# Two fused graph layers: the last batch's projections by seven block products, and buffers of its own for the last pair

## The chip, the cores and the metric

The kernel runs on one core of a Trainium2 chip. The metric is device time in microseconds for one execution, of which the kernel before has three runs (the median is used). The core's engines are TensorE (PE, with its weight loads shown as PEld), VectorE (DVE), ScalarE (ACT), GpSimd (POOL) and SyncE (SP), which here issues the transfers. Each engine works through its own queue in order.

## The reference, cut to what matters

There are 64 graphs of 256 nodes with 256 features. Layer 0 is a convolution over the nodes, a message passing step and a gated update. Layer 1, which is what the change touches, is this (after the layer norm, `h` is the normalised `x`):

```python
def _L1_gnn_ref(x, adj, W_rel, b_rel, W_root, ln_gamma, ln_beta):
    h = layer_norm(x, ln_gamma, ln_beta)
    agg = jnp.einsum('bij,bjh->bih', adj, h)
    conv = jnp.einsum('bkh,ho->bko', agg, W_rel) + b_rel + jnp.einsum('bkh,ho->bko', h, W_root)
    return x + jax.nn.relu(conv)
...
x = _layernorm(x + _L0_gnn_ref(x, adj, ...), axis=-1)
x = _layernorm(x + _L1_gnn_ref(x, adj, ...), axis=-1)
```

Everything is in float32.

## The kernel before, in words

**Tiles and stages.** The 64 graphs are eight batches of eight. Each batch is first convolved over its nodes in a transformed domain (`conv`): the data lie in 48 slots of 128 x 256 in a tile `XF`, whose slots are called `X`, and 47 filter matrices are multiplied in (`product`, `ps_k`, L735), streamed from DRAM through `cs`. Then the batch's graphs are taken in pairs; `pair(p)` records the work of graphs 2p and 2p+1 for p = 0 to 31, so the last batch is the pairs 28 to 31. While one batch's pairs are worked on, the next batch's convolution runs between them; in the last batch there is no next one, and the slots of `X` are unused once the pair's convolved rows have been copied to `XC`.

**A pair** takes these steps, each with the line of its recording:
- messages (`ps_msg`, L1118), distances from node coordinates that make a trip through DRAM (`ps_dist`, L1154), the adjacency `AT` (an exponential on ACT, times the mask on DVE, L1161), and the neighbour sum `nmp` (`ps_nmp`, L1168);
- the gates. Two blocks per side of weights and features are multiplied by seven products in place of eight (Winograd's form of Strassen's method), in the tiles `RG` and `ZN`: `product` L1220 accumulates into PSUM banks `ps_a`, `ps_b`, `ps_d`; `put` copies a bank out on ACT (L1232 for `ZN`, L1234 for `RG`), `onto` adds one on DVE (L1238), `squash` is a tanh (L1242). A bank `ps_a` is used for four products in succession, each accumulated onto the one before, and each must have been copied out before the next starts. Pairs 0, 1 and 31 are "plain": they use eight ordinary products (`ps_g`, L1206);
- the update (L1302 to L1311), which leaves the new state transposed in `wT`;
- `norm`: the statistics of the new state. From pair 2 on, `wT` is turned by a DVE transpose within 32 x 32 blocks (L1328, into `HY`) and two trips through DRAM (`wd`, L1332, and back to `x1`, L1336). In the last batch ("late") the statistics are bn_stats on DVE (`stats`, L1092 and L1093); q and the shift `sh` follow through a power on POOL (L1370) and L1372, and L1376 on ACT scales `x1`;
- `project`: `HY = (wT.T @ [W_rel, W_root]) * q + hrow`, with the two weight matrices side by side in `wrr`. For each graph and half of its nodes (`spots`) there are two matmuls of 128 x 128 by 128 x 512 into `ps_hy` (L1395), and DVE scales the bank into `HY` (L1397);
- `aggregate`: the mask `adja` (loaded at L1315) times the first half of `HY` (`ps_agg`, L1409), an addition (L1412), relu and residual (L1413), statistics, L1428 and L1431 with a power on POOL (L1429), the scaling on ACT (L1438), and the store (L1439).

**The last pair** ("apart") is done block by block. Its graph 0 passes the gates ahead of its graph 1, and each block is finished by `turn_in` (L1247 to L1253: three steps on DVE, two tanh on ACT, then three on DVE). PE transposes `wT` (`ps_wT`, L1350), the projection is L1386 with its scaling L1389, and graph 1's two halves of nodes are aggregated one by one in `last_nodes` (L1448 to L1458).

**What sets the order.** All operations are first recorded as `Op`s with a key, which is a due time computed from the constants at the top: `FIRST_GATES + p * PERIOD` is a pair's due time, `LATE_LAG` shifts the last batch's projections and aggregations behind their own gates, `LOAD_AHEAD` shifts loads, and so on. `scheduled` is a list scheduler with assumed durations, which picks for each engine the ready operation with the smallest key; DVE operations of a pair get a lead. What it returns is the fixed order of each engine's queue, and it also assigns the eight PSUM banks. So a constant changes no operation, only the order in which the operations stand in the queues.

Buffers: `x1`, `HY`, `wT` and `adja` are one tile each, used by all pairs in turn.

Of the kernel before, what the change touches and what calls it, by code (L numbers as in the profile page):

```python
# [18 lines left out]
P = 128  # L19
B, N, D = 64, 256, 256  # L20
C = D // P
# [33 lines left out]
OB, OG = 3, 64  # L55
HQ = 2 * M * C * (M + 1)
XC_SLOTS = BG + 2
FIRST_GATES, PERIOD, GATE_TIME = 112.8, 58.9, 14.5
AHEAD_FROM, AHEAD_TO, W_DEEP = -31.4, -60.1, 2
CONV1_FROM, CONV1_TO, CONV_FROM, CONV_OUT, CONV_TO = -29.4, 98.8, -11.5, -38.6, -37.2  # L60
PAIR_LEAD, FILTER_LEAD, LOAD_AHEAD = 40.4, 0.1, 17.5
SMALL_RUNS, TURN_FROM = 1.3, 2
FILTERS_TO, STORES_AT = 51.4, 46.6
KEEP = 13.0
LATE_LAG = 28.1
W_FROM, W_LAG = 2, 43.3
COORDS = 39.9
PLAIN, SUMS_FROM = (0, 1, B // 2 - 1), 2


# [349 lines left out]
def gnn_two_layers(  # L420
# [18 lines left out]
    prog = Program()  # L439
    PE, V, A, G, SP = prog.tensor, prog.vector, prog.scalar, prog.gpsimd, prog.sync  # L440
# [3 lines left out]
    def sb(name, shape, pool="const"):  # L444
        s = Space(name, shape, pool)
        s.after = opened.get(pool)
        spaces[pool].append(s)
        return s.view

    def ring(name, shape, n, pool="const"):  # L450
        return cycle([sb(f"{name}{i}", shape, pool) for i in range(n)])

    def bank(name, share="rest"):
        return Space(name, [P, 512], "psum", share, share if share in ("conv", "gate") else None).view

    def stt(o, in0, s, in1, op0=ALU.mult, op1=ALU.add, up=1):
        V.scalar_tensor_tensor(o, in0, s, in1, op0=op0, op1=op1, lines_up=up)
# [25 lines left out]
    X = XF[:, :SLOTS * D].rearrange("p (s e) -> p s e", e=D)  # L483
# [494 lines left out]
    wrr = sb("wrr", [P, C, 2 * D])  # L978
    hrow = sb("hrow", [P, 2 * D])
# [58 lines left out]
    wT = sb("wT", [P, 4, N], "work")  # L1038
    x1 = sb("x1", [P, 2, C, D], "work")
    HY = sb("HY", [P, 2, C, 2 * D], "work")  # L1040
    XC = sb("xc", [P, C, XC_SLOTS, N], "work")
    adja = sb("adja", [P, 2, C, N], "work")

    while next(first) != 0:
        pass
# [24 lines left out]
    ps = bank("ps_hrow")  # L1070
# [10 lines left out]
    ps = bank("ps_mean")  # L1081
# [3 lines left out]
    for c in range(C):  # L1085
        stt(wrr[:, c, :], ps, -1.0 / D, wrr[:, c, :])

    mvs, sixes = ring("mv", [P, 4, 2], 2), ring("six", [P, 6], 2)

    def stats(mv, src):  # L1090
        six = next(sixes)
        V.bn_stats(six, src)  # L1092
        V.bn_aggr(mv, six)  # L1093

    qs, q3s = ring("q", [P, 2, 4], 2), ring("q3", [P, 4], 2)
    shs, totals = ring("sh", [P, 4], 4), ring("total", [P, 4], 8)
    sqs, nss = ring("sq", [P, C, 2, 3], 2), ring("ns", [P, C, 2], 2)

    def pair(p):
# [13 lines left out]
        for g in range(2):  # L1113
            for m in range(C):
                ps = bank("ps_msg")
                with prog.group():
                    for c in range(C):
                        PE.matmul(ps[:, :D + 4], xT[:, c, g, m * P:(m + 1) * P], wms[:, c, :], start=(c == 0),  # L1118
                                  stop=(c == C - 1), hold=[msg[:, g, m]])
# [16 lines left out]

        prog.at(due - COORDS, 0.3)
        V.transpose(turned.rearrange("p m e -> p (m e)"), st.rearrange("p m e -> p (m e)"))
# [11 lines left out]
        with prog.group():  # L1150
            for g in range(2):
                for m in range(C):
                    r = slice((2 * g + m) * SR, (2 * g + m) * SR + 4)
                    PE.matmul(pss[2 * g + m][:, :N], lr[r, 0, m * P:(m + 1) * P], lr[r, 1, :], start=True, stop=True,  # L1154
                              hold=[AT[:, g, m]])
# [7 lines left out]
        for g in range(2):  # L1163
            ps = bank("ps_nmp")
            with prog.group():
                for d in range(C):
                    for m in range(C):
                        PE.matmul(ps[:, d * N:(d + 1) * N], msg[:, g, m, d * P:(d + 1) * P], AT[:, g, m, :],  # L1168
                                  start=(m == 0), stop=(m == C - 1), hold=[nmp[:, :, g]])
# [8 lines left out]
        for v, t, when in zip(ins, (tx, nmps, tc_), (due - 28, due - 10, due - 20)):  # L1178
            prog.at(when, 0.3)
            b11, b12, b21, b22 = (v[:, c, g, :] for c in range(C) for g in range(2))  # L1180
# [42 lines left out]

        prog.lead = PAIR_LEAD
        late = p >= B // 2 - BG // 2
        plain = p in PLAIN
        apart = p == B // 2 - 1

# [26 lines left out]
        if plain:  # L1255
            prog.at(due, 2 * GATE_TIME / 44)
            for gs in ((0,), (1,)) if apart else ((0, 1),):
                for T in (RG, ZN):
                    for f in range(C):
                        for g in gs:  # L1260
                            a = bank("ps_g", "gate")
# [8 lines left out]
        else:  # L1270
            for T in (RG, ZN):
                second = T is ZN
                prog.at(due + second * GATE_TIME, GATE_TIME / 21)
                a = bank("ps_a", "gate")
                product(a, 0, second, True)
                put(T, 0, 0, a)
                b_ = bank("ps_b", "gate")
# [4 lines left out]
                d = bank("ps_d", "gate")  # L1282
# [17 lines left out]
        for some in pieces:  # L1300
            r, gh, z, n = (T[:, some, h, :] for T in (RG, ZN) for h in range(2))
# [15 lines left out]
        def spots(gs):  # L1317
            return [(g, m, 2 * g + m) for g in gs for m in range(C)]

        def norm(gs):  # L1320
# [55 lines left out]
                A.activation(x1[:, g, m, :], source[j], AF.Identity, bias=sh[:, j:j + 1], scale=q[:, 0, j:j + 1])  # L1376
            return q

        def project(gs, q):
            prog.at(due + 2 * GATE_TIME + (8 if not apart else -6 if gs[0] else 13 - 2 * GATE_TIME) + (0.0 if apart or p < W_FROM else LATE_LAG if late else W_LAG), 0.6)  # L1380
            if apart:
                pss = [bank("ps_hy") for _ in range(C)]
                for f in range(C):
                    with prog.group():
                        for g, m, j in spots(gs):
                            PE.matmul(pss[m], wT[:, 2 * f + g, m * P:(m + 1) * P], wrr[:, f, :], start=(f == 0),  # L1386
                                      stop=(f == C - 1), hold=[HY[:, g, m]])
                for g, m, j in spots(gs):
                    stt(HY[:, g, m, :], pss[m], q[:, 1, j:j + 1], hrow)  # L1389
                return  # L1390
            for g, m, j in spots(gs):
                ps = bank("ps_hy")
                with prog.group():
                    for f in range(C):
                        PE.matmul(ps, wT[:, 2 * f + g, m * P:(m + 1) * P], wrr[:, f, :], start=(f == 0),  # L1395
                                  stop=(f == C - 1), hold=[HY[:, g, m]], need=[q[:, 1, j:j + 1]])
                stt(HY[:, g, m, :], ps, q[:, 1, j:j + 1], hrow)  # L1397

        def aggregate(gs):
            prog.at(due + 2 * GATE_TIME + (16 if not apart else 14 - 2 * GATE_TIME) + (0.0 if apart or p < W_FROM else LATE_LAG if late else W_LAG), 0.4)  # L1400
            q, sh = next(q3s), next(shs)
# [58 lines left out]
        if apart:  # L1460
            for gs in ((0,), (1,)):
                q = norm(gs)
                project(gs, q)
            aggregate((0,))
            last_nodes()
        else:
            q = norm((0, 1))
            project((0, 1), q)
            aggregate((0, 1))
# [3 lines left out]
    for b in range(NB):  # L1473
        for p in range(b * BG // 2, (b + 1) * BG // 2):
            if p == B // 2 - 1 and p in PLAIN:
                prog.at(FIRST_GATES + (p - 2) * PERIOD, 0.01)
                A21[0] = X[:, :5].rearrange("p s e -> p (s e)")[:, :9 * P].rearrange("p (s g e) -> p s g e", s=3, g=3)
                for s, (src, r) in enumerate(((whhT, 0), (wihT, D), (wihT, 0))):
                    SP.dma_start(out=A21[0][:, s], in_=src[r:r + P].rearrange(
                        "p (g h e) -> p g h e", g=3, h=2)[:, :, 1, :])  # L1480
            pair(p)
            prog.lead = 0.0
            if p + 1 == SUMS_FROM:
                weight_sums(FIRST_GATES + p * PERIOD + 12)
        if b + 1 < NB:
            start, span = FIRST_GATES + b * BG // 2 * PERIOD, BG // 2 * PERIOD
            at1 = len(prog.ops)
            coming = conv(b + 1)
            while next(coming) != "out":
                pass  # L1490
            at2 = len(prog.ops)
            at3 = at2
            while next(coming) != 0:
                pass
            at3 = len(prog.ops)
            spread(at1, at2, start + CONV_FROM, start + span + CONV_OUT)
            spread(at2, at3, start + span + CONV_OUT, start + span + CONV_TO)
            keep(coming, start + span + CONV_TO)
            at3 = len(prog.ops)
            if b + 2 < NB:  # L1500
                conv1(b + 2)
                spread(at3, len(prog.ops), start + CONV1_FROM, start + CONV1_TO)
# [83 lines left out]
```

## Time and profile before

| | before |
|---|---|
| runs, median (lowest to highest) | 1985.53 us (1984.71 to 1985.73) |
| profiled execution, its own time | 1985.06 us |
| its span, first to last instruction | 1983.3 us |
| granted PE clock | 0.999 |
| PE busy, DVE busy, ACT busy | 1968.8, 1714.0, 1009.2 us |
| projection `ps_hy` L1395, PE | 224.3 us in 496 records |
| `ps_agg` L1409, PE | 118.4 us in 504 records |
| scaling L1397, DVE | 124 instructions, 748 ns each |

The profile is of one execution. A float32 matmul appears as two records, its two passes. Busy times of PE are from modelled ends, so that a record is longer (593 ns for 512 columns) than the distance to the next one; the chain of waits gives the distances. Times in a timeline are microseconds from the start of the span.

### The profile page before, as it was taken

The numbers are of one execution on the slowest core, as the hardware profiler recorded it, in microseconds if no ns is written. First come the engines' busy times: TensorE is split into PE (matmuls) and PEld (weight loads), VectorE is DVE, ScalarE is ACT, GpSimd is POOL, SyncE is SP. The second block draws the span as 40 slices with busy tenths as digits, with TensorE's granted clock in tenths as the row PEclk, the third lists the DMA queues.
The fourth block names the chain that finished last, engine by engine and source line by source line (L and its number), as shares of the span: only waits on it lengthen the run. The fifth ranks groups of instructions, "written<-read, shape, count | busy, mean of one in ns | idle before, by whom it ended". The sixth has DMA issues, their size and how long they took to land.

```text
span 1983.3 us, 28889 instructions
## 1 busy us (share of the span) xinstructions
PE 1968.8 (99%) x10196; PEld 1602.8 (81%) x10196; DVE 1714.0 (86%) x2674; ACT 1009.2 (51%) x2342; POOL 290.8 (15%) x512
## 2 busy tenths in 40 slices
PE   9999999999999999999999999999999999999998
PEld 6877789777887788878887788877898788887875
DVE  6996998999999998999989999899988999995655
ACT  7545443654446543664346544475445653456432
POOL 2111110211111111112011111112111010111001
PEclk9999999999999999999999999999999999999999
DMA  8863554446554554445544455544545325422221
GB/s 222 296 209 101 160 155 132 136 114 183 134 153 129 131 181 127 129 141 156 169 142 126 125 146 166 155 131 109 170 136 153 97 81 166 126 73 77 76 54 43
DMA packets 461104, 273.12 MB, mean 138 GB/s; under 512 B 258208, under 2 KB 445600, under 8 KB 460960
## 3 DMA queue, kind: packets, MB, share of 16 engines
q1 hardware_dynamic: 460400, 270.94, 47.7%
q8 instruction: 80, 1.31, 0.3%
q14 instruction: 64, 0.52, 0.1%
q10 hardware_dynamic: 560, 0.34, 0.1%
HBM read 194.01 MB, written 77.20 MB: 137 GB/s over the span
## 4 chain that ended last, share of the span: by engine, by line
PE 96%; ACT 2%; DVE 1%; DMA 1%; issue 0%; SPq 0%; POOLq 0%; POOL 0%; DVEq 0%; ACTq 0%
PE ps_a L1220 23%; PE ps_k L735 17%; PE ps_d L1220 11%; PE ps_hy L1395 11%; PE ps_b L1220 6%; PE ps_nmp L1168 6%; PE ps_agg L1409 5%; PE ps_msg L1118 5%; PE ps_c L879 5%; PE ps_g L1206 4%; PE ps_dist L1154 1%; ACT w2all L596 1%; ACT tT L571 1%; DMA cs<-w2m 0%; PE ps_hy L1386 0%
## 5 line engine op out<-in xcount | busy, mean ns | idle before, releaser
L735 PEld LDWEIGHTS ps_k<-XF,cs 128*128 128x128 f32 x2632 | 311.1, 192 | 15.5 <-issue 10.2
L735 PE MATMUL ps_k<-XF,cs 128*128 128x128 f32 x2632 | 313.1, 275 | 0.0
L1395 PE MATMUL ps_hy<-wrr,wT 128*128 128x512 f32 x496 | 224.3, 593 | 0.0
L1220 PE MATMUL ps_a<-nmp,WB 128*128 128x256 f32 x696 | 207.0, 379 | 0.0
L1395 PEld LDWEIGHTS ps_hy<-wrr,wT 128*128 128x128 f32 x496 | 92.3, 190 | 93.0 <-issue 86.5
L1220 PE MATMUL ps_a<-tx,WB 128*128 128x256 f32 x522 | 155.2, 381 | 2.0 <-ACT ZN L1232 2.0
L1232 ACT COPY ZN<-ps_a 128x512 f32<-128x512 f32 x116 | 67.7, 584 | 172.4 <-PE ps_a L1220 172.0
L1220 PEld LDWEIGHTS ps_a<-nmp,WB 128*128 128x128 f32 x696 | 132.2, 190 | 18.0
L1234 ACT ACTIVATE RG<-ps_a,bhh 128x512 f32<-128x512 f32 x116 | 79.2, 683 | 122.8 <-PE ps_a L1220 120.3
L707 DVE TENSOR_TENSOR XF<-XF 128x512 f32<-128x512 f32 (+3 forms) x128 | 126.6, 1010 | 8.5 <-ACT XF L788 6.6
L1118 PE MATMUL ps_msg<-wms,xT 128*128 128x260 f32 x512 | 133.2, 383 | 0.0
L1397 DVE SCALAR_TENSOR_TENSOR HY<-ps_hy,q,hrow 128x512 f32<-128x512 f32 x124 | 92.8, 748 | 36.3 <-PE ps_hy L1395 22.1
L1168 PE MATMUL ps_nmp<-AT,msg 128*128 128x256 f32 x512 | 119.1, 379 | 0.0
L1409 PE MATMUL ps_agg<-HY,adja 128*128 128x256 f32 x504 | 118.4, 379 | 0.0
L1409 PEld LDWEIGHTS ps_agg<-HY,adja 128*128 128x128 f32 x504 | 95.1, 190 | 25.7 <-issue 14.4
L1220 PEld LDWEIGHTS ps_a<-tx,WB 128*128 128x128 f32 x522 | 96.2, 190 | 23.8 <-issue 7.4
L1423 POOL TENSOR_SCALAR total<-total 128x4 f32<-128x4 f32 x28 | 13.4, 478 | 655.7 <-ACT HY L1419 640.1
L1168 PEld LDWEIGHTS ps_nmp<-AT,msg 128*128 128x128 f32 x512 | 96.8, 190 | 13.8 <-DVE AT L1161 0.5
L1118 PEld LDWEIGHTS ps_msg<-wms,xT 128*128 128x128 f32 x512 | 94.8, 190 | 14.5 <-issue 2.4
L879 PE MATMUL ps_c<-xTc,w 128*128 128x512 f32 x232 | 106.3, 593 | 0.0
L1220 PE MATMUL ps_a<-xc,WB 128*128 128x256 f32 x348 | 103.5, 379 | 0.0
L1220 PE MATMUL ps_a<-tc,WB 128*128 128x256 f32 x348 | 103.5, 379 | 0.0
(227 smaller groups left out, 4360.1 us busy)
## 6 DMA issues: line engine op xcount, KB each, us to landing
cs<-w2m SPq DMA_DIRECT2D x105, 768.0 KB
adjm<-in_adjT_dram SPq DMA_DIRECT2D x64, 256.0 KB
xT<-xt SPq DMA_DIRECT2D x32, 512.0 KB
adja<-in_adjT_dram SPq DMA_DIRECT2D x64, 256.0 KB
out_dram<-HY SPq DMA_DIRECT2D x63, 256.0 KB
hd<-xn SPq DMA_DIRECT2D x28, 544.0 KB
XF<-hd SPq DMA_DIRECT2D x28, 544.0 KB
xt<-xTc SPq DMA_DIRECT2D x29, 512.0 KB
```

Of the source, the lines that this page charges most:

```text
L707: (V.tensor_add if add else V.tensor_sub)(sl(o, n), sl(a, n), sl(b, n))
L735: PE.matmul(ps[:, o * P:(o + 1) * P], w(m, c)[:, o * P:(o + 1) * P], X[:, slot, c * P:(c + 1) * P], start=first and o == 0 and c == 0, sto ...
L879: PE.matmul(ps, w1[:, c, o * P:(o + 1) * P], xTc[:, c, :], start=(c == 0), stop=(c == C - 1), hold=[h[:, :, o]])
L1118: PE.matmul(ps[:, :D + 4], xT[:, c, g, m * P:(m + 1) * P], wms[:, c, :], start=(c == 0), stop=(c == C - 1), hold=[msg[:, g, m]])
L1168: PE.matmul(ps[:, d * N:(d + 1) * N], msg[:, g, m, d * P:(d + 1) * P], AT[:, g, m, :], start=(m == 0), stop=(m == C - 1), hold=[nmp[:, :, g]])
L1206: PE.matmul(ps[:, h * N:(h + 1) * N], block[:, s, gate, :], right[s][2 * k + g], start=0 in ks and h == 0 and s == sources[0] and k == 0, ...
L1220: PE.matmul(ps[:, h * N:(h + 1) * N], block[:, s, gate, :], right[s][at], start=start and h == 0 and j == 0, stop=j == len(sources) - 1, s ...
L1232: A.copy(o, ps)
L1234: A.activation(o, ps, AF.Identity, bias=bhh[:, 2, f:f + 1])
L1395: PE.matmul(ps, wT[:, 2 * f + g, m * P:(m + 1) * P], wrr[:, f, :], start=(f == 0), stop=(f == C - 1), hold=[HY[:, g, m]], need=[q[:, 1, j: ...
L1397: stt(HY[:, g, m, :], ps, q[:, 1, j:j + 1], hrow)
L1409: PE.matmul(ps[:, n_ * D:(n_ + 1) * D], adja[:, g, m, n_ * P:(n_ + 1) * P], HY[:, g, m, :D], start=(m == 0), stop=(m == C - 1))
```

## The change

Three things change together.

1. For the pairs from `SEVEN_FROM` = 28 on, other than the last, `project` calls the new `seven_products`: the 2 x 2 blocks of `wT` and of `wrr` are multiplied by seven block products of 256 columns. Sums of weight blocks are made once (`wrr_sums`), differences of state blocks for each pair; they lie in free slots of `X` (29 to 36). The products go to three banks (`ps_ha` four times, `ps_hb`, `ps_hd` twice), are copied or added into `HY`, and `HY` is scaled in place.
2. In the last pair, `x1`, `HY`, `wT` and `adja` are slots 8 to 27 of `X`; the rings of small tiles (`mv`, `six`, `q`, `q3`, `sh`) are longer.
3. Fifteen or so of the constants that make the keys have other values, so that the queues' orders differ.

```diff
-FIRST_GATES, PERIOD, GATE_TIME = 112.8, 58.9, 14.5
-AHEAD_FROM, AHEAD_TO, W_DEEP = -31.4, -60.1, 2
-CONV1_FROM, CONV1_TO, CONV_FROM, CONV_OUT, CONV_TO = -29.4, 98.8, -11.5, -38.6, -37.2
-PAIR_LEAD, FILTER_LEAD, LOAD_AHEAD = 40.4, 0.1, 17.5
+FIRST_GATES, PERIOD, GATE_TIME = 111.7, 58.8, 14.3
+AHEAD_FROM, AHEAD_TO, W_DEEP = -31.2, -63.8, 2
+CONV1_FROM, CONV1_TO, CONV_FROM, CONV_OUT, CONV_TO = -25.7, 97.3, -11.5, -38.6, -36.1
+PAIR_LEAD, FILTER_LEAD, LOAD_AHEAD = 40.4, -0.5, 19.5
 SMALL_RUNS, TURN_FROM = 1.3, 2
-FILTERS_TO, STORES_AT = 51.4, 46.6
+FILTERS_TO, STORES_AT = 50.9, 52.3
 KEEP = 13.0
-LATE_LAG = 28.1
+LATE_LAG = 38
 W_FROM, W_LAG = 2, 43.3
-COORDS = 39.9
+COORDS = 43.5
+SEVEN_FROM = B // 2 - 4
...
+    SHARED = x1, HY, wT, adja
...
+    made_sums = []
+
+    def wrr_sums():
+        a11, a12, a21, a22 = (wrr[:, k, f * D:(f + 1) * D] for f in range(2) for k in range(C))
+        s2, s4, s5, s6 = (X[:, i] for i in range(29, 33))
+        if not made_sums:
+            kept = prog.key, prog.step
+            prog.at(FIRST_GATES + SEVEN_FROM * PERIOD + 40, 0.01)
+            V.tensor_add(s4, a21, a22)
+            V.tensor_sub(s5, s4, a11)
+            V.tensor_sub(s6, a11, a21)
+            V.tensor_sub(s2, a12, s5)
+            prog.at(*kept)
+            made_sums.append(1)
+        return a11, a12, s2, a22, s4, s5, s6
+
-    mvs, sixes = ring("mv", [P, 4, 2], 2), ring("six", [P, 6], 2)
+    mvs, sixes = ring("mv", [P, 4, 2], 6), ring("six", [P, 6], 12)
...
-    qs, q3s = ring("q", [P, 2, 4], 2), ring("q3", [P, 4], 2)
-    shs, totals = ring("sh", [P, 4], 4), ring("total", [P, 4], 8)
+    qs, q3s = ring("q", [P, 2, 4], 4), ring("q3", [P, 4], 4)
+    shs, totals = ring("sh", [P, 4], 8), ring("total", [P, 4], 8)
...
+        x1, HY, wT, adja = SHARED
+        if p == B // 2 - 1:
+            x1 = X[:, 8:12].rearrange("p (g m) d -> p g m d", g=2)
+            HY = X[:, 12:20].rearrange("p (g m h) d -> p g m (h d)", g=2, m=C)
+            wT, adja = X[:, 20:24], X[:, 24:28].rearrange("p (g c) n -> p g c n", g=2)
...
+        def seven_products(q):
+            b11, b12, b21, b22 = (wT[:, i] for i in range(4))
+            t = X[:, 33:37]
+            V.tensor_sub(t[:, 0:2], wT[:, 1:4:2], wT[:, 0:2])
+            V.tensor_sub(t[:, 2], b22, t[:, 0])
+            V.tensor_sub(t[:, 3], b21, t[:, 2])
+            blocks = (b11, b21, b22, t[:, 3], t[:, 0], t[:, 2], t[:, 1])
+            w_ = wrr_sums()
+
+            def one(ps, i, start):
+                with prog.group():
+                    for m in range(C):
+                        PE.matmul(ps[:, m * D:(m + 1) * D], blocks[i][:, m * P:(m + 1) * P], w_[i],
+                                  start=start and m == 0, stop=True, skip_group_check=True,
+                                  hold=[HY] if i == 0 else [], need=[q[:, 1]] if start else [])
+
+            def place(f, g, ps, add):
+                o, v = HY[:, g, :, f * D:(f + 1) * D], ps.rearrange("p (m d) -> p m d", m=C)
+                V.tensor_add(o, o, v) if add else A.copy(o, v)
+            a = bank("ps_ha")
+            one(a, 0, True)
+            place(0, 0, a, False)
+            b_ = bank("ps_hb")
+            one(b_, 1, True)
+            place(0, 0, b_, True)
+            one(a, 5, False)
+            place(0, 1, a, False)
+            d = bank("ps_hd")
+            one(d, 4, True)
+            one(a, 6, False)
+            place(1, 1, a, False)
+            place(1, 1, d, True)
+            one(d, 2, False)
+            place(0, 1, d, True)
+            one(a, 3, False)
+            place(1, 0, a, False)
+            for g, m, j in spots((0, 1)):
+                stt(HY[:, g, m], HY[:, g, m], q[:, 1, j:j + 1], hrow)
...
+            if p >= SEVEN_FROM:
+                seven_products(q)
+                return
```

## The prediction

> **What bounds the kernel now.** I read the profile's page first: TensorE (PE) is busy 99% of the span, VectorE (DVE) 86%, and DVE falls to five or six tenths in the last slices, where no convolution is left.
>
> ```profile
> PE 1968.8 (99%) x10196; PEld 1602.8 (81%) x10196; DVE 1714.0 (86%) x2674; ACT 1009.2 (51%) x2342; POOL 290.8 (15%) x512
> DVE  6996998999999998999989999899988999995655
> ```
>
> A busy PE may still hide gaps, so next comes the table of busy time by stretch, and against it the sum of PE's work from the chain of waits (a 256-column pass every 0.216 us, a 512-column one every 0.43). From 145.6 us, PE's one wait of 1.4 us behind the weight set-up (`ps_mean`), to the end of its last unbroken run at 1972, the passes sum to 1817 of 1826 us. What is missing is some 31 times 0.19 us behind `ps_dist` (the products after its small matmuls take 2.35 in place of 2.16) and three stalls of 0.9 us. So the middle has nothing to win, and any new wait of PE there is paid in full.
>
> ```profile
> 150.00:1780.00 1630.00, 1629.33 (x8315) 1334.95 (x8314) 1464.14 (x2215) 832.62 (x1974) 243.41 (x427) 1.00 0.48 137
> 1930.00:1984.00 54.00, 44.37 (x176) 32.11 (x174) 29.37 (x85) 14.12 (x28) 6.82 (x7) 0.96 0.17 47
> ```
>
> (Line numbers are always those of the kernel before. Columns: stretch, length, then busy time and count of PE, PEld, DVE, ACT, POOL, then PE's clock.) Then the chain of waits, in order of time (start, length, what), around the change and to the end:
>
> ```profile
> 1862.85 3.45 PE ps_agg L1409 x16
> ...
> 1911.80 0.59 ACT ZN L1232
> 1912.39 0.04 issue
> 1912.44 2.43 PE ps_a L1220 x10
> ...
> 1943.76 6.87 PE ps_hy L1395 x16
> ...
> 1958.62 4.32 PE ps_g L1206 x20
> ...
> 1980.00 0.60 ACT HY L1457
> ```
>
> Eight projection matmuls of 512 columns (16 passes) take 6.87 us; 16 passes of 256 take 3.45; and where a bank's next product follows directly on the one that ACT must first copy out, PE stands. Last, DVE's timeline (start, length, instruction) for how its instructions follow one another at the end:
>
> ```profile
> 1970.51 0.69 DVE L1412 TENSOR_TENSOR HY<-HY,ps_agg 128x512 f32<-128x512 f32 x1 [1.55 <-PE ps_agg L1409]
> 1971.31 0.69 DVE L1413 SCALAR_TENSOR_TENSOR HY<-HY,x 128x512 f32<-128x512 f32 x1
> 1972.04 0.43 DVE L1092 BATCH_NORM_STATS2 six<-HY 128x6 f32<-128x256 f32 x1
> ...
> 1973.24 0.17 DVE L1428 TENSOR_SCALAR q<-mv 128x2 f32<-128x2 f32 x1
> 1973.32 0.15 DVE L1372 SCALAR_TENSOR_TENSOR sh<-mv,q 128x2 f32<-128x2 f32 x1
> 1973.39 1.40 DVE L1389 SCALAR_TENSOR_TENSOR HY<-ps_hy,q,hrow 128x512 f32<-128x512 f32 x2
> ```
>
> Add, relu, four statistics and the small step take 2.7 us of DVE per graph; two evictions of 512 take 1.3.
>
> **1. The products.** Per pair 16 passes of 512 (6.87) become 28 of 256: 28 x 0.216 = 6.04 us. That is 0.83 less, in pairs 28, 29 and 30: **-2.49 us**, all of it PE time. Here a rule speaks against it: the Trainium skill ("TensorE: Matmul & The Clock Gate", Back-to-back issue gap) says that spacing is set by weight load and matmul together, 81 ns at 128 columns and 131 at 512. Interpolated to 98 ns at 256, an estimate, 28 would cost 2.7 against 2.1 and the three pairs would lose 1.9 us; this trace's 256- and 512-column rows are strictly proportional.
>
> **2. What the products add elsewhere.** Per pair on DVE: three differences (0.69 + 2 x 0.42), three additions from PSUM (0.69 each) and four scalings from SBUF in place of four from PSUM (0.7 each, even); on ACT four copies of 0.58; once, four sums of weights (0.42 each). In pairs 28 and 29 DVE (30 of 50 us busy) and ACT (20 of 50) take this beside PE: 0. But each `ps_ha` copy stands between two products of one bank, and what is queued on PE behind a waiting product waits too. In the built order other matmuls lie between, at least one 0.86 us product, against a copy of 0.58 and two handovers. That just fits in pair 29's projection; there, though, a copy also comes between ACT's four exponentials, and pair 31's `ps_nmp` follows `ps_dist` by 2.6 us with an `AT` that I reckon 0.25 late, 0.45 with the restart: **+0.45** (0 to 2.8, three full stalls).
>
> **3. The gates' own adjacency.** In the built order of before a gate product follows its own bank's copied one three times; after, four times. Each costs 0.65 waiting and 0.27 (2.43 against 2.16) restarting: **+0.92**.
>
> **4. The constants.** PE's order is the same through pair 4's gates, so the filters are untouched; a few swaps differ up to pair 9, then the distances from `ps_dist` to `ps_nmp` and from `ps_hy` to `ps_agg` repeat those of before. SP's queue is reshuffled from the 79th transfer (a filter load ahead of the `hd` store, `sd` ahead of `xn` and `XF`); the wait at 145.6 is DVE's queue and stays. I take 0; below by 0.4 (all that is unexplained in the middle), above by 1.4, one such wait.
>
> **5. The last pair's buffers.** They free pair 31 from pair 30's `wT`, `HY`, `x1`, `adja`. No wait of PE in the trace is for these: the mask was issued at 1962.2 and used at 1968.6 without one. By itself 0. What it allows is the new order, with `LATE_LAG` 38: pair 30's projection and aggregation are interleaved with pair 31's gates and last steps. One step is moved in DVE's queue: pair 30's transpose (L1328) stood at 1926.8, before pair 31's `turn_in`; now it is behind the first of them, some 7.5 us later, and its two trips through DRAM (9.8 us before, transpose's end to landing) bring `x1` at about 1945.4. Its statistics stand in DVE's queue ahead of pair 31's first evictions, whose products PE ends at 1947.2, so there is a margin of about 1 us: I take 0, up to 2 if the transfers slip.
>
> **6. The end.** Count from the last gate product. Before it ends at 1962.78 (start of the next instruction) and the span at 1983.3: 20.5 us. Behind it lie 11.0 us of PE work before and 13.4 after (two of pair 31's projections, 3.44, have moved ahead; three of pair 30's products, 2.59, and its two aggregations, 3.45, have come behind, less 0.2 of transposes). So after it ends earlier by 2.40 + 2.49 - 0.92 - 0.45 = 3.5 us, at 1959.3. From there, in the built order, with the steps just shown (us behind that point):
>
> - DVE and ACT turn the last block (L1248 to L1253, done at 3.4); PE's last `ps_ha` ends at 3.7, ACT's copy at 4.45. From here DVE no longer waits.
> - first scaling, four statistics and two small steps on the last `ps_wT`, the `ps_hd` addition, two scalings: 4.5 to 8.4.
> - graph 0 of pair 31 (add, relu, four statistics, small): to 11.2.
> - two evictions of graph 1, pair 30's first add between: to 13.2. `ps_agg` L1448 needs both, and waits 3.3 us on PE.
> - graph 0 of pair 30, rest: to 15.1; the fourth scaling: 15.7; node half 0 of graph 1: 17.45; node half 1's add: 17.8.
> - graph 1 of pair 30: to 20.4; node half 1's relu and statistics: 21.7; POOL's power (0.55) and the shift: 22.6.
> - ACT has pair 30's four scalings (2.06) queued in front of the last L1457: from 22.0 to 24.6. Before, the end came 2.7 behind that instruction; with two 256 KB stores just ahead I add 0.4: 27.7.
>
> The last node half before had DVE almost for itself; now pair 30's 10 us of late work stand in its queue. The end grows from 20.5 to 27.7: **+7.2 us** (26.3 if stores and handovers cost nothing, 29 if each of ten handovers costs 0.13 more).
>
> **Sum.** -3.5 + 7.2 = +3.7 on the span of 1983.3, so 1987.0; the profiled execution took 1985.06, 1.8 outside the span, and the median of the runs is 1985.53, 0.5 above that: 1985.53 + 3.7 = **1989.2 us**.
>
> **The rivals.** *DVE keeps up and the end stays PE's* (not slower): if DVE clears pair 30's scalings and first aggregate before the last gate product, PE ends at 1959.3 + 13.4 + 0.2 = 1972.9; then 2.7 (graph), 1.3 (power and shift), 2.1 (ACT), 2.7 (store): 1981.7, so -1.6, 1983.9. It decides once DVE's unbroken queue behind the last gate product is 5.3 us shorter than I counted (13 in place of 18 us); against it, all those steps stand in one queue in the order above, and only a wrong duration could shorten it. *PE waits in the projections too*: three stalls of 0.92 more, or `x1` 2 us late, give 1991 to 1992. For it, the margins of 0.1 and 1 us; against, ACT is 40% busy there. *The seven products do not save*: with loads in the way, +2.5 on my sum, 1991.7; 256-column rows speak against it. *Something in the middle is faster*: the accounting leaves 0.4 us, so I know no mechanism; if I misread DVE's end as well, 1981.
>
> **Chances.** My case 0.60, the PE-bound end 0.15, waits in the projections 0.18, an unseen gain 0.07. A measurement of this kernel tells about 0.2%, 4 us, from no change. My case straddles +4 us, nearly half of it above; the second lies within, the third above: faster 0.07, same 0.47, slower 0.46. The range reaches from most of the PE-bound end to the late `x1`: 1984.5 to 1992.0; my case's own is 1987.2 to 1991.2.
>
> **What would show it.** Right: `ps_ha`, `ps_hb`, `ps_hd` at 0.216 us a pass; four PE waits on `ZN` L1232; PE's wait before the last-node `ps_agg` grown from 2.0 to about 3.3 and now on DVE; DVE without idle time over its last 18 us; the last gate product near 1959. Wrong: that product above 1961 (waits in the projections), or DVE idle in the last 15 us and the span below 1984.

## The result and the profile after

Eleven runs of the changed kernel have a median of 1990.37 us (1989.75 to 1991.12), eleven of the kernel before, on the same chip, 1985.23 us (1984.71 to 1985.96). The ratio is 1.0025, with a 95% interval of 1.0017 to 1.0034: slower by 5.1 us, beyond the 0.2% that can be told from no change, if not by much. The forecast was 1989.2, in the range 1984.5 to 1992.0; the likeliest case, slower at the end of the run, is what happened. The profiled execution has a span of 1988.5 us (before 1983.3).

The code has shifted: `ps_a` L1220 is L1238 in the kernel after, `ZN` L1232 is L1255, the first add of the aggregation L1412 is L1477, the last pair's eviction L1389 is L1451 and its last aggregation L1448 is L1513. New are L1414 (the seven products), L1420 (their copies and additions) and L1439 (the scalings).

The page first, busy time and DVE by slices:

```profile
PE 1968.4 (99%) x10232; PEld 1609.9 (81%) x10232; DVE 1726.2 (87%) x2696; ACT 1017.2 (51%) x2354; POOL 282.1 (14%) x512
```

PE is as busy as before although its passes fell by 2.5 us of work (near the end it ran at half its clock for a while, see the last section), and DVE has 12 us more. The table of busy time by stretch (stretch, length, then busy time and count of PE, PEld, DVE, ACT, POOL, and PE's clock):

```profile
150.00:1780.00 1630.00, 1628.81 (x8311) 1334.04 (x8310) 1466.12 (x2216) 833.80 (x1972) 233.95 (x425) 1.00 0.49 138
1930.00:1989.00 59.00, 46.11 (x192) 36.07 (x190) 32.44 (x91) 18.51 (x37) 7.24 (x8) 0.91 0.20 54
```

The long middle is what it was, to half a microsecond. The last stretch has 1.7 us more of PE, 3.1 more of DVE and 4.4 more of ACT, and is 5 us longer. The chain of waits shows the new products and the new end:

```profile
1907.94 0.86 PE ps_ha L1414 x4
1908.80 0.86 PE ps_hb L1414 x4
...
1956.20 4.32 PE ps_g L1224 x20
1960.52 0.22 PE ps_wT L1373 x2
...
1981.55 1.20 POOL q L1494
1982.76 0.02 issue
1982.78 0.17 DVE sh L1496
1982.95 0.02 issue
1982.98 1.09 ACT HY L1503 x2
```

Four passes of a product take 0.86 us, 0.216 each, as reckoned. The last gate product ends at 1960.5 (before, by the same view, 1962.9), and from there it is 28.0 us to the end (before 20.4). So the front has gained 2.4 and the end has lost 7.6. On that end DVE's timeline (start, length, instruction, idle time before it and what ended it):

```profile
1972.83 0.75 DVE L1451 SCALAR_TENSOR_TENSOR XF<-ps_hy,q,hrow 128x512 f32<-128x512 f32 x1
...
1975.37 0.72 DVE L1439 SCALAR_TENSOR_TENSOR HY<-HY,q,hrow 128x512 f32<-128x512 f32 x1
...
1978.65 0.69 DVE L1477 TENSOR_TENSOR HY<-HY,ps_agg 128x512 f32<-128x512 f32 x1 [0.50 <-PE ps_agg L1474]
...
1983.40 0.16 DVE L1521 SCALAR_TENSOR_TENSOR sh<-mv,q 128x1 f32<-128x1 f32 x1 [0.45 <-POOL q L1520]
```

Pair 30's scaling (L1439) and aggregation (L1477) stand between the last pair's steps, and from 1964.8 on DVE has two idle moments worth a line, 0.50 and 0.45 us. Last PE's waits from 130 us to the end (what, on what, us in total, times, longest):

```profile
PE ps_a L1238 <- ACT ZN L1255: 3.6, 5, 1.0
PE ps_agg L1513 <- DVE XF L1451: 2.5, 2, 1.9
PE ps_mean L1086 <- DVE wrr L1082: 1.4, 1, 1.4
PE ps_d L1238 <- DVE ZN L1261: 0.2, 1, 0.2
```

Before, the same view had the last-node aggregation waiting on ACT's `x1`, and three waits on `ZN`:

```profile
PE ps_agg L1448 <- ACT x L1376: 2.0, 1, 2.0
PE ps_a L1220 <- ACT ZN L1232: 2.0, 3, 0.7
```

### The profile page after: what moved, and what is told of

Read it like the earlier page. It is cut to its first block, busy times and chain, and to the rows that moved or that the text cites. A ratio compares the mean times of both kernels' runs of the same rounds, so it can differ in the third digit from the quotient of the medians.

```text
span 1988.5 us, 28994 instructions
## 1 busy us (share of the span) xinstructions
PE 1968.4 (99%) x10232; PEld 1609.9 (81%) x10232; DVE 1726.2 (87%) x2696; ACT 1017.2 (51%) x2354; POOL 282.1 (14%) x512
## 4 chain that ended last, share of the span: by engine, by line
PE 93%; ACT 2%; DVE 1%; DMA 1%; SPq 1%; issue 1%; POOL 0%; ACTq 0%; DVEq 0%
PE ps_a L1238 22%; PE ps_k L736 17%; PE ps_d L1238 11%; PE ps_hy L1460 10%; PE ps_nmp L1186 6%; PE ps_b L1238 5%; PE ps_msg L1136 5%; PE ps_agg L1474 5%; PE ps_c L880 5%; PE ps_g L1224 4%; ACT w2all L597 1%; PE ps_dist L1172 1%; PE ps_ha L1414 1%; ACT tT L572 1%; DMA x<-wd 0%
## 5 line engine op out<-in xcount | busy, mean ns | idle before, releaser
L1238 PE MATMUL ps_a<-nmp,WB 128*128 128x256 f32 x696 | 207.0, 379 | 0.0
L1460 PE MATMUL ps_hy<-wrr,wT 128*128 128x512 f32 x448 | 204.1, 594 | 0.0
L1238 PE MATMUL ps_a<-tx,WB 128*128 128x256 f32 x522 | 155.7, 381 | 3.6 <-ACT ZN L1255 3.6
L1460 PEld LDWEIGHTS ps_hy<-wrr,wT 128*128 128x128 f32 x448 | 83.2, 190 | 82.1 <-issue 77.7
L1238 PEld LDWEIGHTS ps_a<-nmp,WB 128*128 128x128 f32 x696 | 132.2, 190 | 18.0
L1255 ACT COPY ZN<-ps_a 128x512 f32<-128x512 f32 x116 | 67.5, 582 | 134.9 <-PE ps_a L1238 134.9
L1238 PEld LDWEIGHTS ps_a<-tx,WB 128*128 128x128 f32 x522 | 96.0, 190 | 26.0 <-issue 7.2
L1462 DVE SCALAR_TENSOR_TENSOR HY<-ps_hy,q,hrow 128x512 f32<-128x512 f32 x112 | 83.6, 748 | 30.2 <-PE ps_hy L1460 20.5
L1238 PE MATMUL ps_a<-xc,WB 128*128 128x256 f32 x348 | 103.5, 379 | 0.0
L1238 PE MATMUL ps_d<-nmp,WB 128*128 128x256 f32 x348 | 103.5, 379 | 0.0
```

The lines of the kernel that those rows point to most:

```text
L1238: PE.matmul(ps[:, h * N:(h + 1) * N], block[:, s, gate, :], right[s][at], start=start and h == 0 and j == 0, stop=j == len(sources) - 1, s ...
L1255: A.copy(o, ps)
```

## The experiments

Three theories were set against each other. **End-of-queue**: what stands in DVE's and ACT's queues behind the last gate product sets the end, and the seven products harm by what of theirs stands there. **Products**: their copies, additions and scalings cost wherever they stand. **Constants**: the new order of the whole run costs something, whatever the products do.

To compare runs I cut each profiled execution at two marks of the chain of waits: the start of the last ordinary projection before the change begins (pair 27's `ps_hy`, at 1815.63 before) and the end of the last gate product. "DVE behind" is DVE's busy time from that end on, from the table of busy time by stretch.

| run | median us | ratio to before (95%) | to mark 1 | gates | behind | DVE behind |
|---|---|---|---|---|---|---|
| before | 1985.2 to 1985.6 | | 1815.6 | 147.3 | 20.4 | 13.1 |
| after | 1990.37 | 1.0025 (1.0017 to 1.0034) | 1816.4 | 144.1 | 28.0 | 19.1 |
| e1 buffers | 1989.34 | 1.0019 (1.0009 to 1.0028) | 1816.1 | 151.0 | 19.7 | 10.5 |
| e2 constants | 1993.73 | 1.0041 (1.0026 to 1.0056) | 1816.8 | 142.6 | 32.0 | 18.1 |
| e3 constants, buffers | 1987.84 | 1.0012 (1.0002 to 1.0021) | 1817.2 | 146.4 | 22.4 | 15.1 |
| e4 seven, buffers | 1992.39 | 1.0035 (1.0022 to 1.0048) | 1816.8 | 147.8 | 26.3 | 18.3 |
| e5 after, pair 30 short | 1987.94 | 1.0014 (1.0005 to 1.0023) | 1817.0 | 143.9 | 26.3 | 16.3 |
| e6 after, pair 29 short | 1990.47 | 1.0027 (1.0017 to 1.0036) | 1816.9 | 143.9 | 28.1 | 19.1 |
| e7 seven for 29 | 1991.14 | 1.0030 (1.0018 to 1.0041) | 1816.4 | 151.6 | 21.1 | 11.8 |
| e8 seven for 28, 29 | 1992.68 | 1.0039 (1.0026 to 1.0051) | 1816.5 | 149.9 | 25.4 | 13.6 |
| e9 e7, masks first | 1986.00 | 1.0004 (0.9995 to 1.0013) | 1815.9 | 147.4 | 21.1 | 13.2 |
| e10 seven for 28 | 1989.34 | 1.0023 (1.0014 to 1.0032) | 1815.9 | 150.6 | 20.3 | 13.1 |

The first column of times is of one execution each. With the old constants it lies between 1815.6 and 1816.8, mean 1816.2; with the new ones between 1816.4 and 1817.2, mean 1816.9.

### The three parts apart

All runs keep the longer rings of small tiles. No run has them alone; built with the old constants, they leave the order of every queue as it was before. Run e1 is the kernel before with the last pair's own buffers alone:

```diff
 (constants as before)
+SEVEN_FROM = B // 2
+        if p == B // 2 - 1:
+            x1 = X[:, 8:12]...; HY = X[:, 12:20]...; wT, adja = X[:, 20:24], X[:, 24:28]...
```

> Before, with the last pair's own buffers alone (old constants, no seven products). End-of-queue theory (the time is lost in what stands on VectorE behind the last gate product): behind that product stand 7.3 us of TensorE work in place of 11.0, so it ends near 1966.4, and the end follows some 16 to 17.5 us later: 1982.5 to 1984 in the span, so -1 to +0.5 us. Products theory (the copies and additions of the seven products cost wherever they stand): 0, since there are none. Constants theory (the new order of the whole run costs): 0, since the constants are old.

It took 3.8 us more than before: all three theories missed. PE's waits show it:

```profile
PE ps_agg L1513 <- ACT XF L1399: 4.3, 1, 4.3
```

With its own buffers the order changes even under the old keys: only 7.3 us of PE work stay behind the last gate product (counted in the built order; before 11.0), the rest has moved ahead of it. The gates' stretch is 3.7 us longer for that, but the end is only 0.7 shorter, because the last aggregation still has to wait for the last statistics, now 4.3 us in place of 2.0. Buffers that remove no wait of the trace are not neutral where an order is computed from them.

Run e2 has the new constants alone:

```diff
-LATE_LAG = 28.1
+LATE_LAG = 38
 (and the other constants of the change)
+SEVEN_FROM = B // 2
```

> Before, with the new constants alone. Constants theory: most of the +5.1 us, +3 to +5. End-of-queue theory: both aggregations of pair 30 (3.45 us) move behind the last gate product, 14.7 us of TensorE work in place of 11.0, and two gate products directly behind one of their own bank in place of three (-0.9): -1 if TensorE still sets the end, up to +2 if VectorE does. Products theory: -1 to 0.

It is the slowest of all, +8.2, above all three forecasts. PE's waits near the end, and two lines of its chain of waits:

```profile
PE ps_wT L1369 <- DVE wT L1272: 4.1, 1, 4.1
PE ps_agg L1509 <- DVE HY L1447: 1.9, 1, 1.9
PE ps_agg L1470 <- DVE HY L1447: 1.1, 1, 1.1
```

```profile
1972.96 2.14 DMA out_dram<-HY
...
1975.24 0.76 DVE HY L1447
```

The new order weaves pair 30's and pair 31's last steps into each other, but they share `HY`, `wT` and `x1`: the chain of waits goes through pair 30's store (2.14 us) before the last pair's eviction may write `HY`. The gates' stretch is the shortest of all runs and the end the longest.

Run e3 is the kernel after without the seven products (`SEVEN_FROM = B // 2`).

> The changed kernel without the seven products (new constants, own buffers, eight products of pairs 28 to 30 as before). Products theory: it is as fast as before or faster, -1 to 0, and all the loss is in the products. End-of-queue theory: the last gate product ends near 1962.1 and pair 30's second aggregation and statistics stand behind it on VectorE, an end of 22 to 24 us: +1 to +3. Constants theory: +4 to +5.

+2.3, where end-of-queue had it. With e1 and e2 this shows that the constants and the buffers belong together: the buffers cost 3.8 alone, the constants 8.2 alone, both 2.3. To the kernel after it lacks only the products: they shorten the gates' stretch by 2.3 us and lengthen the end by 5.6 (22.4 to 28.0), while DVE's busy time behind the last gate product grows by 4.0 (15.1 to 19.1). So of the 7.6 us by which the end is longer than before, 2.0 are there without the products (20.4 to 22.4).

Run e4 is the kernel after with the old constants.

> The changed kernel with the old constants. Constants theory: the products' gain is left, -2.5 to -1. End-of-queue theory: 12.5 us of TensorE work behind the last gate product, which ends near 1960.6, and an end of 25 to 27 us: +2 to +4. Products theory: +4 to +5, as with the new constants.

+6.8, above all three. The end (26.3) is where end-of-queue had it, but the last gate product comes at 1964.6 and not near 1960.6. PE's waits:

```profile
PE ps_agg L1513 <- DVE XF L1451: 5.7, 1, 5.7
PE ps_a L1238 <- ACT ZN L1255: 3.8, 4, 1.3
PE ps_ha L1414 <- ACT HY L1420: 1.6, 2, 1.1
PE ps_agg L1474 <- DVE HY L1439: 0.9, 1, 0.9
```

Here the products cost in the middle too (`ps_ha` stands on its own copies, an aggregation on the scalings), so with products and buffers in, the new constants are worth 1.7 us (+5.1 in place of +6.8).

### DVE's work behind the last gate product, and elsewhere

Run e5 takes pair 30's late DVE work away in part; run e6 takes the same from pair 29, whose aggregation lies 40 us earlier. The assumed durations are pinned, so that all queues keep their order.

```diff
-                y = HY[:, g, :, D:]
-                V.tensor_add(y, y, ps...)
-                stt(y, y, 0.0, x1[:, g], ...)
+                y, few = HY[:, g, :, D:], 32 if p == B // 2 - 2 else D      # e6: B // 2 - 3
+                V.tensor_add(y[:, :, :few], y[:, :, :few], ps...[:, :, :few])
+                stt(y[:, :, :few], y[:, :, :few], 0.0, x1[:, g, :, :few], ...)
...
-                        stats(mv[:, j, :], y[:, m, :])
+                        stats(mv[:, j, :], y[:, m, :few])
```

> The kernel after, in which pair 30's aggregation handles only 32 of 256 columns of each half of nodes in its DVE steps (addition, relu and residual, statistics): 224 columns are left out, and every queue keeps its order. By the trace of after a DVE step of 512 takes 0.69 us and one of 256 takes 0.42, so at 64 the four steps should save about 0.45 each, the four statistics about 0.25 each: 2.8 us, all of it behind the last gate product. End-of-queue theory: the span falls by 2.3 to 2.8 us, to 1985.7 to 1986.2, and the last gate product still ends near 1960.4. Products theory (the copies and additions of the seven products cost wherever they stand): these are all still there, so the time stays within 0.5 us of after (about +5 on before).

> The control to the run before it: the same columns left out of the same DVE steps, but of pair 29's aggregation (in the trace of after from 1924 to 1929 us), with every queue in the order of after. About 2.8 us of DVE work less, beside PE's gates and not behind the last gate product. End-of-queue theory: 0 to -0.4 us against after. If DVE's work as a whole were the limit of the last batch: -2 to -2.8 us.

e5 took 1987.94, e6 1990.47, the kernel after 1990.37. DVE's busy time behind the last gate product fell by 2.8 in e5, as reckoned, and the time by 2.5 against its control, as end-of-queue had it; the same work taken away 40 us earlier is worth nothing. This is end-of-queue's case, and against products: in both runs every product, copy and addition is in place. e5's profiled execution is the slowest of its eleven (1988.95 us); its end is 1.8 shorter than the control's. Its chain still goes through pair 30's last aggregation on PE and through POOL, as the one of after does, so those two are part of this end as well:

```profile
1975.99 2.50 PE ps_agg L1474 x8
...
1980.02 1.21 POOL q L1494
```

### The seven products away from the end

In runs e7 to e10 the products are added to the kernel before, with old constants and shared buffers (lines are 4 lower than after). e7 has them for pair 29 alone, e8 for 28 and 29.

```diff
-            if p >= SEVEN_FROM:
+            if SEVEN_FROM + 1 == p:            # e8: SEVEN_FROM <= p < B // 2 - 2
                 seven_products(q)
```

> The kernel before with seven products for pair 29 alone, old constants, shared buffers. PE's passes: -0.83. In the built order a gate product follows its own bank's copied one twice (before three times): -0.92. Behind the last gate product lie 10.8 us of PE work (before 11.0): the product ends 0.2 later. Sum: last gate product at 1961.2 to 1961.3 (before 1962.8). Behind it the last pair's first two evictions have come behind its graph 1's statistics, which brings its first aggregate some 0.7 us later. End-of-queue theory: -0.9 us on before (-1.7 to 0). Products theory (a third of the +2.8 us that three pairs cost): +0.9.

> The kernel before with seven products for pairs 28 and 29, old constants, shared buffers. PE's passes: -1.66. In the built order a gate product follows its own bank's copied one four times (before three) and a ps_ha product once: +0.92 and +0.9. PE work behind the last gate product 11.2 us (before 11.0): -0.2. Sum: last gate product at 1962.6 (before 1962.8). Behind it, as with pair 29 alone, the first aggregate some 0.7 us later. End-of-queue theory: +0.6 us on before (-0.5 to +1.5). Products theory (two thirds of +2.8): +1.9.

+5.9 and +7.4: far off for both theories; end-of-queue in its strict form, that only the end counts, falls here. PE's wait in e7, and DVE's queue ahead of it:

```profile
PE ps_nmp L1186 <- DVE AT L1179: 3.9, 1, 3.9
```

```profile
1910.77 2.74 DVE L1435 SCALAR_TENSOR_TENSOR HY<-HY,q,hrow 128x512 f32<-128x512 f32 x4
...
1914.76 0.68 DVE L1473 TENSOR_TENSOR HY<-HY,ps_agg 128x512 f32<-128x512 f32 x1
...
1919.98 1.29 DVE L1179 TENSOR_TENSOR AT<-AT,adjm 128x512 f32<-128x512 f32 x2
```

Pair 31's mask stands behind pair 29's four scalings and its whole aggregation, and PE stands at `ps_nmp` for it. So DVE's queue can be late in the middle as well, at a place that my count of work (30 of 50 us busy) did not show. In the kernel after the mask is at 1912.4, ahead of pair 29's aggregation, which the new constants put at 1924:

```profile
1912.40 1.42 DVE L1179 TENSOR_TENSOR AT<-AT,adjm 128x512 f32<-128x512 f32 x2 [1.94 <-ACT AT L1176]
...
1924.09 0.68 DVE L1477 TENSOR_TENSOR HY<-HY,ps_agg 128x512 f32<-128x512 f32 x1
```

e8 loses less there (0.3), but 2.9 on the last pair's `wT`, 1.6 on `ps_ha` and 0.9 on an aggregation.

That leaves a wider form of it, the queue theory: the products cost what their copies, additions and scalings push back in any queue that PE then waits for. Run e9 tests it; it is e7 with one line, which makes these masks more urgent in the scheduler:

```diff
-            V.tensor_mul(AT[:, g], AT[:, g], adjm[:, g])
+            V.tensor_mul(AT[:, g], AT[:, g], adjm[:, g]); prog.ops[-1].urgent += 60.0 * (p >= B // 2 - 2)
```

> The kernel with seven products for pair 29 alone (which took 1991.1, +5.9 on before, and whose PE stood 3.9 us at ps_nmp for pair 31's AT, whose mask stood in DVE's queue behind pair 29's scalings and its whole aggregation). Here DVE's mask products of pairs 30 and 31 are recorded as more urgent; in the built order pair 31's now stand before pair 29's last relu and statistics, and the order behind the last gate product is that of before again. Queue theory (the seven products' copies, additions and scalings cost what they push back in DVE's queue and PE then waits for): ps_nmp's wait falls to about 1.3, the last pair's 0.7 goes: -3.3 us, to 1987.8 (+2.5 on before; 1987 to 1988.5). If the products themselves cost wherever they stand: as without this edit, 1991.

It took 1986.00, better than the 1987.8 expected: 5.1 us of e7's 5.9 go, and the time can't be told from before. `ps_nmp` still waits:

```profile
PE ps_nmp L1186 <- DVE AT L1179: 1.8, 1, 1.8
```

The edit also changed the order behind it (the last pair's as before, and PE's work behind the last gate product), so not all of the 5.1 is the mask: 2.1 are the wait, and a wait of 0.9 on the last `wT` is gone.

Run e10 moves the products to pair 28.

> The kernel before with seven products for pair 28 alone: beside pair 29's and 30's gates, 50 us further from the end, with the queue behind the last gate product as in before. PE's passes -0.83; a gate product follows its own bank's copied one four times (before three): +0.92. In the built order pair 30's masks stand ahead of pair 28's scalings, and pair 31's behind pair 29's aggregation as in before. Queue theory: +0.1 us on before (-0.6 to +1.2). If the products cost wherever they stand, as pair 29's did: +3 to +6.

+4.1, queue theory's +0.1 missed. PE's waits:

```profile
PE ps_a L1238 <- ACT ZN L1251: 3.2, 4, 1.1
PE ps_nmp L1186 <- DVE AT L1179: 2.2, 2, 1.9
PE ps_ha L1410 <- ACT HY L1416: 0.5, 1, 0.5
```

The end is that of before to 0.1 us; of the 3.5 us that the profiled execution loses, 3.3 lie in the gates. Pair 31's masks stand behind pair 29's aggregation in DVE's queue as they do before, but on PE two gate products (4.3 us) that stood between that aggregation and `ps_dist` have come ahead of it, and nothing covers the 1.9 us any more. The chains of waits show it, before:

```profile
1906.15 3.45 PE ps_agg L1409 x16
1909.61 2.17 PE ps_a L1220 x10
...
1914.86 0.64 PE ps_dist L1154 x8
```

and in e10:

```profile
1903.49 2.43 PE ps_a L1238 x10
1905.91 6.87 PE ps_hy L1456 x16
1912.78 1.74 PE ps_agg L1470 x8
```

That this order costs the wait is read from the traces; no run tests it. I had looked at DVE's order and not at the cover on PE.

Together: a product takes its 0.86 us on PE in every run, and no run keeps the saving; the waits and the longer ends shown above take it back. None of the versions run is faster than the kernel before; the nearest is e9. Not tried were a version with an order made by hand for the last batch, and the new constants one by one.

## Why the prediction was right, and where it was off

**1, the products.** Right: 0.216 us a pass (one of the two records of a matmul) at L1414, so 28 passes take 6.04 us in place of 6.87. The rule of the Trainium skill ("TensorE: Matmul & The Clock Gate", Back-to-back issue gap), by whose two figures, taken as a line (an estimate), 256 columns would cost more than half of 512, does not hold for these float32 passes.

**2 and 3, the waits in the gates.** Nearly right: between the marks the gates gained 3.2 us where 3.5 were reckoned. Two waits on `ZN` of 0.7 stand there (before one), as counted, and `ps_nmp` took 1.97 for 1.73, so 0.25 where 0.45 was reckoned. Put at nothing was `ps_d`: it waited 0.2 on DVE at 1905 and then took 2.43 in place of 2.16.

**4, the constants.** 0 was taken, from -0.4 to +1.4, and this is the step that was too small: the last gate product was reckoned at 1959.3 and ended at 1960.4, 1.1 later, and 0.8 of it is there at mark 1 already, ahead of any product. A fifth wait on `ZN`, of 0.5 between 400 and 800 us, is new. The five runs with the new constants all have it (0.3 to 0.6), the seven with the old ones do not. The rest is the wait near 1811 us, 1.0 and not 0.7, because eight statistics on ACT (1.70) stand in front of the copy and waited for pair 27's transfers; it is 1.0 to 1.3 in every run but before, with the old constants too, so this part is not theirs. The profiled executions of the new constants reach mark 1 0.7 later in the mean, half of the upper bound.

**5, the buffers, and `x1` of pair 30.** The margin of 1 us did not hold on DVE: `x1` landed at about 1947.6, 2.2 later than reckoned, DVE stood 1.6 us for it, and the last pair's first two evictions began at 1950.1, 1.6 behind the second one's product. PE did not stand for them, so the 0 came true without the margin. That the buffers cost nothing by themselves was wrong as a statement on them alone (e1: +3.8). Constants and buffers together, without the products, cost 2.3 (e3); the prediction had no price for this by itself, and counted what they move behind the last gate product under 6.

**6, the end.** Right, and nearly step by step. From the last gate product (1960.36, start of the next instruction):

| step | reckoned | measured |
|---|---|---|
| last `ps_ha` copied on ACT | 4.45 | 4.45 |
| scalings, statistics, `ps_hd` done | 8.4 | 8.4 |
| graph 0 of pair 31 | 11.2 | 11.2 |
| two evictions of graph 1 | 13.2 | 13.1 |
| fourth scaling | 15.7 | 15.7 |
| graph 1 of pair 30 | 20.4 | 21.1 |
| ACT starts pair 30's scalings | 22.0 | 22.6 |
| last scaling ends | 24.6 | 25.2 |
| end | 27.7 | 28.1 |

The one slip is DVE's idle 0.50 ahead of graph 1 of pair 30, whose aggregation on PE ran at half its clock (below). One wait came smaller than forecast: PE's in front of the last-node `ps_agg` is 2.5 in two and not 3.3, because two passes ran behind the first eviction alone and did not need both. In sum -2.4 and +7.6 make +5.2 on the span, against -3.5 and +7.2. e5 and e6 show that DVE's work at this end sets the time: 2.8 us of it taken away give 2.5.

**The rivals.** The end bound by PE: no, DVE's queue was not shorter than counted. Waits in the projections: between the marks the gates gained 3.2 us where 3.5 were reckoned, so 0.3 of the 2.8 that this rival priced, and PE never stood at `ps_ha`. "Seven products do not save": no. What no rival named is that the same products lose 4 to 7 us under the old constants (e7, e8, e10), largely by waits of PE on the queues of DVE and ACT ahead of the last gate product.

## What to carry to other kernels

On an engine that is busy 99% of the span, as PE is here, a saving arrives only if the last engine to finish has less to do behind it: count the other engines' work behind the bottleneck's last independent piece before the saving itself, step by step from the built queues. Where an order is computed, a change of buffers or work reorders everything near it, so judge parts only in the combination that will run, and look at the place of the longest-waited operation in each queue (here the mask) and at what covers it on PE. Constants that are harmful alone (e2) can be what makes the change bearable (e4 against after).

## What the runs showed of the hardware

PE's clock falls to half after short waits, sometimes. In the kernel after, PE waited 1.9 us and 0.6 us for the last evictions; the table of busy time by stretch, in the kernel after, the last columns being clock, DMA share and GB/s:

```profile
1968.00:1970.00 2.00, 2.00 (x11) 1.77 (x10) 1.97 (x4) 0.00 (x0) 0.05 (x1) 1.00 0.00 0
1975.00:1977.00 2.00, 2.00 (x6) 1.44 (x5) 1.83 (x6) 0.00 (x0) 0.00 (x0) 0.50 0.39 131
1977.00:1978.00 1.00, 1.00 (x3) 0.78 (x3) 0.93 (x4) 0.00 (x0) 0.10 (x1) 0.51 0.00 0
```

At 0.50 the eight passes of pair 30's last aggregation took 2.93 us in place of 1.73. In the same place the kernel before ran at 1.00 behind a wait of 2.0 us (four passes in the chain: 1.32 us), and e9 at 0.50 behind the same wait of 2.0 us (2.06):

```profile
1974.50:1976.60 2.10, 2.07 (x5) 1.69 (x6) 0.66 (x2) 1.47 (x3) 0.00 (x0) 0.50 0.00 0
```

The Trainium skill ("TensorE: Matmul & The Clock Gate", Part 1, "What's actually happening") puts the fall to half rate at an idle window of about 3.4 us that runs freely, without regard to the kernel; a wait of 2.0 us was enough here. That the window runs freely would fit the two outcomes of one wait, but no run here shows it. What the runs show is how long the half clock lasts. Cut into pieces of 0.2 us, the same table has it from 1974.6 to 1978.0 in the kernel after, and nine such stretches in seven runs (after, e2, e3, e5, e6, e8, e9) all last 3.4 us before the full clock comes back. The price at this end was some 0.5 us, as DVE's idle time shows.
